# Cross-attention on one core: the order in which probabilities are split and multiplied by the values, and what the fill loads when

## The chip, the cores and the metric

The kernel runs on one core of a Trainium2 chip. The metric is the device time of one execution in microseconds (us). Five engines work side by side, each through its own instructions in the order in which they were issued: TensorE (PE, with its weight loads shown as PEld), VectorE (DVE), ScalarE (ACT), GpSimd (POOL) and SyncE (SP, which here issues nearly all DMAs). They wait for one another through semaphores.

## The reference

```python
q = heads(hidden @ to_q_w)                        # x: 32 batches x 512 rows x 640; 20 heads of 32
k, v = heads(ctx @ to_k_w), heads(ctx @ to_v_w)   # ctx: 32 x 77 keys x 1024
out = merge(softmax(q k^T / sqrt(32)) v) @ to_out_w + to_out_b + hidden
```

The other branches of the reference (object, other and image keys) have no keys in these inputs: all 77 keys are text. All is float32. The kernel splits each operand of a product into a high part in fp32r and the rest ("low") and adds three products: high by high, high by low, low by high.

## The kernel before

**Stages.** First all 32 batches' keys and values are computed and left in DRAM scratch (`k_dram`, `v_dram`), as are the split output weights (`wo_dram`). The main part then goes through 160 *slots*: slot `n = 5 b + j` handles batch `b` and a block `j` of four heads (128 of the 640 columns), for all 512 rows, in four row tiles `t`. After them, `end()` drains the pipeline. The order of all instructions is written by hand (`tc.manual_schedule`), so what `slot` says first is issued first on each engine. Buffers' waits are made by the tile pools.

**What a slot does.** It works for several heads blocks at once:

- PE: `scores(n, t)` for t = 0 to 3 (three matmuls each, tile `sc`), the queries of the next slot (`queries`, 15 matmuls, `pq`), the values product of slot `n - 4` (`values`, six matmuls of 512 columns, `pa`), and 24 output matmuls of an earlier batch in two *pieces* (`project` by `piece`, tile `po`). In slots with j = 1 and j = 4 the first piece stands before the fourth scores ("early").
- DVE: the negated maximum of the scores (`nm`, inside `scores`), `rest_p` (the low part of the probabilities, 128 x 1024), `sums` (the reciprocal `rs` of the softmax sums of slot n - 1), `low_a` (the low part of the attention output `at` of slot n - 5), `split_q`'s two low parts, the transposition `z` of the probabilities, the additions to the output (`finish`) and to `pa` (`sum_a`), transposes of the next batch's `x` (`xs`).
- ACT: `cast_p` (two casts of `raw` to the high part `pp`: 128 x 1024, and the last 64 key rows, 64 x 512), `high_a` (`at` high), four `exps` per row tile, `split_q`'s high part, `sum_a`'s copy, and casts of the next `x` (`split_x`).
- POOL: `copy_keys` (j = 1 and 4), `last_p` (low part of the last 64 rows, 64 x 512), `normalize` (multiplies the probabilities of slot n - 1 by `rs`, 128 x 1232), two casts of `split_q`, `add_bias`, low parts of `split_x`.
- SP: all loads and stores, among them `pd<-z` and its way back, `raw<-pd` (`load_p`), the keys (`load_keys`, `kb`), the values (`load_values`, `vb`), `x`, residuals and outputs. Each DMA of SP waits until the one issued eight before it has landed, as the build's order with its waits shows.

The probabilities take the way `pn` (exps, normalize), `z`, DRAM `pd`, `raw`, `pp`. A product of values reads `pp` in six passes: `pp[:, 0:2]` is the high part of 128 rows by two, `pp[:, 2:4]` their rest, and `pp[:, 4]` holds the high part of the last 64 rows in its lower half and the low part in its upper half.

The lines behind the steps below: L458, L462 and L464 `split_q`, L482 `scores`, L490 `nm`, L500 `exps`, L510 `sums`, L515 `normalize`, L522 `z`, L538 and L539 `load_p`, L546 and L547 `cast_p`, L553 `rest_p`, L560 `last_p`, L577 `values`, L588 and L590 `sum_a`, L597 `high_a`, L602 `low_a`, L621 `project`, L658 `finish`, L427 and L428 `copy_keys`, L447 `queries`, L264 and L265 `split_x`, L257 `transpose_x`, L412 the clearing of `vb`.

**The fill.** Slots 0 to 2 also carry the last value products of the context (`beside`). Slot 4 is the first that takes a product of values, slot 8 the first with output pieces. The order in a slot is this (cut):

```python
        if taken is not None:
            cast_p(taken)
        if n - 1 in takes:
            high_a(takes[n - 1])
        s = scores(n, 0)
        if taken is not None:
            rest_p(taken)
        rs = sums(n - 1) if n else None
        if taken is not None:
            last_p(taken)
        if n:
            normalize(n - 1, rs)
        if n - 1 in takes:
            low_a(takes[n - 1])
        exps(n, 0, *s)
        queries(n + 1, 0, 2)
        s = scores(n, 1)
```

Of the kernel before, what the change touches and what calls it, by code (L numbers as in the profile page):

```python
# [8 lines left out]
F32 = mybir.dt.float32  # L9
# [14 lines left out]
P = 128  # L24
# [27 lines left out]
def kernel(  # L52
# [325 lines left out]
    for round_ in (range(3), range(3, NC_)):  # L378
        for k in range(NK):
            for j in round_:  # L380
                keys(LAST, j, k)
        for j in round_:
            split_keys(LAST, j)
        if j == 2:
            load_x(1)
    psk.release()
# [10 lines left out]
    bias = main.tile([P, C], F32, name="bias")  # L397
    nc.sync.dma_start(bias, bo.unsqueeze(0).to_broadcast([P, C]))
    kbs, vbs, pnb = [], [], []
# [10 lines left out]
    for g, (j0, nj) in enumerate(GROUPS):  # L410
        vb = main.tile([P, nj, 2, 2, P], FPR, name=f"vb{g}")
        nc.gpsimd.memset(vb.bitcast(F32), 0.0)  # L412
        vbs.append(vb)
# [128 lines left out]
    def cast_p(n):  # L542

        raw = raws[n]
        pp = late[0].tile([P, 5, S], FPR, tag="pp", name="pp", bufs=1)
        nc.scalar.copy(pp[:, 0:2, :], raw[:, 0:2, :])  # L546
        nc.scalar.copy(pp[:64, 4, :], raw[:64, 2, :])  # L547
        pps[n] = pp

    def rest_p(n):  # L550

        raw, pp = raws[n], pps[n]
        nc.vector.tensor_tensor(  # L553
            pp[:, 2:4, :], raw[:, 0:2, :], pp[:, 0:2, :].bitcast(F32), ALU.subtract
        )

    def last_p(n):

        raw, pp = raws.pop(n), pps[n]
        nc.gpsimd.tensor_tensor(  # L560
            pp[64:, 4, :], raw[:64, 2, :], pp[:64, 4, :].bitcast(F32), ALU.subtract
        )

    PASSES = [(p, 0, p + c) for c in (0, 2) for p in range(2)] + [(p, 1, 4) for p in range(2)]

    def values(n, m0=0, m1=6):
        b, j = divmod(n, NC_)
        g = GROUP_OF[j]  # L570
        pp, vb = pps[n], vbs[g][:, j - GROUPS[g][0]]
        if m1 == 6:
            pps.pop(n)
        if m0 == 0:
            pas[n] = late[1].tile([P, 2, S], F32, tag="pa", name="pa", bufs=1)
        for p, t, c in PASSES[m0:m1]:
            nc.tensor.matmul(  # L577
# [3 lines left out]
                start=(c == p),  # L581
                stop=(t == 1),
            )
# [33 lines left out]

    def project(b, t, h, j, m0=0, m1=3):
        for m in range(m0, m1):
            a, c = PAIRS[m]  # L620
            nc.tensor.matmul(  # L621
# [5 lines left out]
            )  # L627

    def close_first(b, n):

        for m0, m1, v0, v1 in ((0, 2, 0, 4), (2, 3, 4, 6)):
            for h in range(2):
                project(b, 0, h, NC_ - 1, m0, m1)
            values(n, v0, v1)
        closed.extend(((b, 0, 0), (b, 0, 1)))

# [41 lines left out]

    WO = {1: (0,), 2: (1,), 3: (2,), 4: (3,), 5: (4,)}
    wos = []  # L680
# [22 lines left out]
    def slot(n, beside=()):  # L703
# [3 lines left out]
        bo_, has_out = b - back, b >= back  # L707
        xsplits = SPLIT_X.get(j, ((), ())) if more and n > 2 else ((), ())
        turns = TRANSPOSE_X.get(j, ((), (), ())) if more and b else ((), (), ())
        taken = takes.get(n)  # L710

        filling = taken is not None and not has_out
        if not filling:
            refill(b, j, 0)
        if j == 1:
            copy_keys(1)
        elif j == 4 and more:
            copy_keys(0)
        if taken is not None:
            cast_p(taken)  # L720
        if n - 1 in takes:
            high_a(takes[n - 1])
        bias_now = j in BIAS and b >= BIAS[j][0]
        if bias_now and not ahead:
            add_bias(b - BIAS[j][0], BIAS[j][1])
        s = scores(n, 0)
        if j == 2:
            finish()
        if taken is not None:
            rest_p(taken)  # L730
        rs = sums(n - 1) if n else None
        if taken is not None:
            last_p(taken)
        if n:
            normalize(n - 1, rs)
        if n - 1 in takes:
            low_a(takes[n - 1])
        exps(n, 0, *s)
        if ahead:
            queries(n + 1, 0, 2)  # L740
        s = scores(n, 1)
        if n >= LATE:
            load_p(n - LAG + 1)
# [16 lines left out]
        if not ahead:  # L760
            exps(n, 2, *s)
            close_first(bo_, taken)
            finish()
            s = scores(n, 3)
        early = ahead and has_out and j in (1, 4)
        if early:
            if j == 4:
                close_first(bo_, taken)
            else:
                piece(bo_, first)  # L770
            finish()
# [47 lines left out]
    def end():  # L819
# [8 lines left out]
        cast_p(N - 4)  # L828
        high_a(N - 5)
        rest_p(N - 4)  # L830
        transpose_p(N - 1)
        low_a(N - 5)
        last_p(N - 4)
        add_bias(last - 1, 2)
# [9 lines left out]
        def turn(n):  # L844
            sum_a(n)
            cast_p(n + 1)
            high_a(n)
            rest_p(n + 1)
            low_a(n)
            last_p(n + 1)  # L850

# [56 lines left out]

    load_keys(0, 0)
    copy_keys(0)  # L910
    queries(0, 0, NC_)
    split_q(0)
    context_values(LAST, 0, psv)
    for i in range(NQ):
        transpose_x(1, i)
    for c in range(2):
        split_x(1, c)
    context_values(LAST, 1, psv)
# [55 lines left out]
```

## Time and profile before

| | us |
|---|---|
| median of 3 runs | 1942.67 (1941.25 to 1948.3) |
| profiled execution | 1943.7, of which the span from first to last instruction is 1941.9 |
| PE busy | 1893.9 (98% of the span) |
| DVE, ACT, POOL busy | 1568.0, 1536.8, 1391.0 |
| mean granted TensorE clock | 0.994 |
| DMA | 431.37 MB, 222 GB/s on average |

In the page, "PE 1893.9 (98%)" means that matmuls were under way for 98% of the span. Matmul ends are modelled, and a matmul that starts late because its operand came late still lengthens what follows, so idle time alone understates what waiting costs. A slot's length is read from the timeline as the distance of the first matmul of `scores(n, 0)` from that of the next slot.

### The profile page before, as it was taken

What the parts mean: (1) busy time and instruction counts of PE and PEld (TensorE: products, weight loads), DVE (VectorE), ACT (ScalarE), POOL (GpSimd) and SP (SyncE); (2) the same over time, 40 slices, a digit from 0 to 9 for tenths busy, and PEclk for the clock granted to TensorE, in tenths of its full rate; (3) what the DMA queues carried; (4) which work ended last, traced back from release to release, by engine and by line L of the source; (5) the groups of instructions that cost most, each with busy time, mean ns of one, the idle gap of its engine ahead of it and who ended that gap; (6) DMA issues with size and microseconds to landing.
All of it is one profiled execution on the core that took longest, in us unless ns stands there. A gap on an engine that the chain in (4) does not pass through costs nothing. (4 is left out here: it accounts for less than half of the span.)

```text
span 1941.9 us, 37554 instructions
## 1 busy us (share of the span) xinstructions
PE 1893.9 (98%) x10332; PEld 1668.6 (86%) x10332; DVE 1568.0 (81%) x2494; ACT 1536.8 (79%) x6210; POOL 1391.0 (72%) x1116
## 2 busy tenths in 40 slices
PE   9999997999999999999999999999999999999998
PEld 7888885888888888888888888888888888888887
DVE  5444446888889888889889888888888888988885
ACT  3232247899988988888998889999989898898883
POOL 1100066888888888788887888888888888888883
PEclk9999998999999999999999999999999999999999
DMA  9888769888888888888888898888888888888875
GB/s 190 206 190 249 186 156 232 217 226 231 233 225 224 225 230 234 225 231 229 231 228 235 233 237 226 231 231 233 221 237 230 222 229 231 229 226 229 235 204 169
DMA packets 565023, 431.37 MB, mean 222 GB/s; under 512 B 191120, under 2 KB 473168, under 8 KB 564816
## 3 DMA queue, kind: packets, MB, share of 16 engines
q1 hardware_dynamic: 560304, 414.47, 82.8%
q0 software_dynamic: 4416, 14.34, 2.3%
q8 instruction: 85, 1.39, 0.3%
q14 instruction: 122, 1.00, 0.2%
q10 hardware_dynamic: 96, 0.16, 0.0%
HBM read 247.17 MB, written 181.64 MB: 221 GB/s over the span
## 5 line engine op out<-in xcount | busy, mean ns | idle before, releaser
L500 ACT ACTIVATE pn<-sc,nm 128x77 f32<-128x77 f32 x2560 | 802.0, 335 | 129.3 <-DVE nm L490 121.4
L621 PE MATMUL po<-wo_s,at 128*128 128x320 f32 x3840 | 637.6, 314 | 10.8 <-ACT at L597 9.8
L447 PE MATMUL pq<-xt,wq_s 128*128 128x512 f32 x2400 | 630.5, 402 | 3.3 <-POOL xt L265 0.2
L621 PEld LDWEIGHTS po<-wo_s,at 128*128 128x128 f32 x3840 | 571.3, 189 | 21.4 <-ACT at L597 15.2
L500 ACT ACTIVATION_READ_ACCUMULATOR pn<-sc,nm 128x1 f32 x2560 | 546.9, 214 | 0.0
L447 PEld LDWEIGHTS pq<-xt,wq_s 128*128 128x128 f32 x2400 | 428.1, 190 | 89.2 <-POOL xt L265 16.2
L515 POOL TENSOR_TENSOR pn<-pn,rs 128x1232 f32<-128x1232 f32 x160 | 363.9, 2274 | 53.5 <-DVE rs L510 43.3
L482 PEld LDWEIGHTS sc<-kb,qt 128*128 128x128 f32 x1920 | 329.4, 189 | 69.0 <-POOL qt L462 13.9
L560 POOL TENSOR_TENSOR pp<-raw,pp 64x512 fp32r<-64x512 f32 x160 | 290.6, 1816 | 131.2 <-ACT pp L547 112.8
L482 PE MATMUL sc<-kb,qt 128*128 128x154 f32 (+1 forms) x1920 | 323.4, 275 | 18.7 <-POOL qt L462 7.0
L464 DVE TENSOR_TENSOR qt<-pq,qt 64x512 fp32r<-64x512 f32 x320 | 220.2, 688 | 111.4 <-ACT qt L458 106.4
L490 DVE TENSOR_REDUCE nm<-sc 128x4 f32<-128x308 f32 x640 | 291.2, 459 | 19.8 <-PE sc L482 13.4
L577 PE MATMUL pa<-pp,vb 128*128 128x512 f32 x960 | 263.3, 404 | 8.1 <-DVE at L602 3.0
L522 DVE STREAM_TRANSPOSE z<-pn 128x1280 f32<-128x1280 f32 x160 | 241.8, 1511 | 8.6 <-DMA pd<-z 2.5
L590 DVE TENSOR_TENSOR pa<-pa,aw 64x512 f32<-64x512 f32 x320 | 222.5, 695 | 19.3 <-ACT aw L588 8.9
L553 DVE TENSOR_TENSOR pp<-raw,pp 128x1024 fp32r<-128x1024 f32 x160 | 203.7, 1273 | 32.6 <-ACT pp L546 32.4
L265 POOL TENSOR_TENSOR xt<-xs,xt 128x512 fp32r<-128x512 f32 x160 | 202.5, 1291 | 33.5 <-ACT xt L264 30.8
L462 POOL CAST qt<-qt 64x512 fp32r<-64x512 f32 x320 | 194.9, 609 | 31.9 <-ACT qt L458 14.1
L613 POOL TENSOR_TENSOR xr<-xr,bias 128x640 f32<-128x640 f32 x128 | 202.2, 1580 | 17.5 <-DMA xr<-in_x_dram 6.1
L577 PEld LDWEIGHTS pa<-pp,vb 128*128 128x128 f32 x960 | 171.9, 189 | 46.7 <-DVE at L602 15.1
L546 ACT CAST pp<-raw 128x1024 fp32r<-128x1024 f32 x160 | 168.7, 1055 | 42.7 <-DMA raw<-pd 40.9
L588 ACT COPY aw<-pa 64x1024 f32<-64x1024 f32 x160 | 161.9, 1012 | 20.1 <-PE pa L577 16.0
(46 smaller groups left out, 1594.0 us busy)
## 6 DMA issues: line engine op xcount, KB each, us to landing
pd<-z SPq DMA_DIRECT2D x640, 160.0 KB, 3.4
raw<-pd SPq DMA_DIRECT2D x160, 512.0 KB, 4.0
xs<-in_x_dram SPq DMA_DIRECT2D x128, 320.0 KB, 7.3
xr<-in_x_dram SPq DMA_DIRECT2D x128, 320.0 KB, 3.7
out_dram<-xr SPq DMA_DIRECT2D x127, 320.0 KB, 3.6
raw<-pd SPq DMA_DIRECT2D x160, 128.0 KB, 4.2
v_dram<-vs SPq DMA_DIRECT2D x80, 192.0 KB, 4.0
k_dram<-ks POOLq DMA_DIRECT2D x20, 512.0 KB, 4.4
```

The costliest lines, as they stand in the source:

```text
L447: nc.tensor.matmul(pqs[n], wq_s[:, k, a, j * P : (j + 1) * P], xts[b, k][:, c, :], start=(k == 0 and m == 0), stop=(k == NC_ - 1 and m == 2),)
L464: nc.vector.tensor_tensor(qt[r, 1 + w, :], pq[r], qt[r, 0, :].bitcast(F32), ALU.subtract)
L482: nc.tensor.matmul(sc[:, cols], qt[:, m, t * P : (t + 1) * P], keys_, start=(m == 0), stop=(m == 2),)
L490: nc.vector.tensor_reduce(nm, sc[:, :KCOLS].rearrange("p (h k) -> p h k", k=NKEY), AX.X, ALU.max, negate=True)
L500: nc.scalar.activation(pnb[n % 2][:, at, :NKEY], sc[:, i * NKEY : (i + 1) * NKEY], AF.Exp, bias=nm[:, i : i + 1], accum_out=sms[n][:, at : ...
L515: nc.gpsimd.tensor_tensor(pf, pf, rs.unsqueeze(2).to_broadcast([P, NQ * HPC, NKEY]), ALU.mult)
L522: nc.vector.transpose(z.rearrange("p b t j -> p t b j"), pn.rearrange("p (t h) k -> p t (h k)", t=NQ).rearrange("p t (b i) -> p t b i", i=Q),)
L553: nc.vector.tensor_tensor(pp[:, 2:4, :], raw[:, 0:2, :], pp[:, 0:2, :].bitcast(F32), ALU.subtract)
L560: nc.gpsimd.tensor_tensor(pp[64:, 4, :], raw[:64, 2, :], pp[:64, 4, :].bitcast(F32), ALU.subtract)
L577: nc.tensor.matmul(pas[n][:, p, :], vb[:, p, t, :], pp[:, c, :], start=(c == p), stop=(t == 1),)
L590: nc.vector.tensor_tensor(pa[64 * p : 64 * p + 64, 0], pa[:64, p], aw[:, p], ALU.add)
L621: nc.tensor.matmul(pos[b, t, h][:, :HALF], ats[b * NC_ + j][:, a, t * P : (t + 1) * P], wos[0][:, j, c, h * HALF : (h + 1) * HALF], start= ...
```

## The change

In every slot the last 64 rows of the probabilities are cast first (`cast_p`), their low part is taken before the rest of the 128-row part, and `rest_p` moves from before `sums` to after `scores(n, 1)`. The six passes of `values` go high, last rows, rest, where they went high, rest, last rows. `low_a` moves behind `rest_p`, except in slots with j = 4, where `high_a` is issued before `cast_p` and `low_a` before `scores(n, 1)`. `close_first`, which interleaved the two closing output products with the values product in those slots, is replaced by the piece and then the product. Slots without output issue `copy_keys` after `last_p`. In the fill, `x` of batch 1 is loaded after the first keys and is transposed and split within slots 0 to 3; the bias is loaded in slot 3; the five parts of the output weights come in slots 1 and 2 instead of 1 to 5; and `vb` is cleared after the first `copy_keys`. `end()` follows the new order of `last_p` and `rest_p`.

```diff
-        if j == 2:
-            load_x(1)
...
-    nc.sync.dma_start(bias, bo.unsqueeze(0).to_broadcast([P, C]))
...
-        nc.gpsimd.memset(vb.bitcast(F32), 0.0)
...
+        nc.scalar.copy(pp[:64, 4, :], raw[:64, 2, :])
         nc.scalar.copy(pp[:, 0:2, :], raw[:, 0:2, :])
-        nc.scalar.copy(pp[:64, 4, :], raw[:64, 2, :])
...
-    PASSES = [(p, 0, p + c) for c in (0, 2) for p in range(2)] + [(p, 1, 4) for p in range(2)]
+    PASSES = [(p, t, c + p * (t == 0)) for t, c in ((0, 0), (1, 4), (0, 2)) for p in range(2)]
...
-    def close_first(b, n):
-
-        for m0, m1, v0, v1 in ((0, 2, 0, 4), (2, 3, 4, 6)):
-            for h in range(2):
-                project(b, 0, h, NC_ - 1, m0, m1)
-            values(n, v0, v1)
-        closed.extend(((b, 0, 0), (b, 0, 1)))
...
-    WO = {1: (0,), 2: (1,), 3: (2,), 4: (3,), 5: (4,)}
+    WO = {1: (0, 1, 2), 2: (3, 4)}
...
-        xsplits = SPLIT_X.get(j, ((), ())) if more and n > 2 else ((), ())
-        turns = TRANSPOSE_X.get(j, ((), (), ())) if more and b else ((), (), ())
+        xsplits = SPLIT_X.get(j, ((), ())) if more else ((), ())
+        turns = TRANSPOSE_X.get(j, ((), (), ())) if more else ((), (), ())
...
-        if j == 1:
-            copy_keys(1)
-        elif j == 4 and more:
-            copy_keys(0)
-        if taken is not None:
+        copied = {1: 1, 4: 0 if more else None}.get(j)
+        if has_out and copied is not None:
+            copy_keys(copied)
+        if taken is not None and j != NC_ - 1:
             cast_p(taken)
         if n - 1 in takes:
             high_a(takes[n - 1])
+        if taken is not None and j == NC_ - 1:
+            cast_p(taken)
...
         s = scores(n, 0)
         if j == 2:
             finish()
-        if taken is not None:
-            rest_p(taken)
         rs = sums(n - 1) if n else None
         if taken is not None:
             last_p(taken)
+        if not has_out and copied is not None:
+            copy_keys(copied)
         if n:
             normalize(n - 1, rs)
-        if n - 1 in takes:
-            low_a(takes[n - 1])
         exps(n, 0, *s)
         if ahead:
             queries(n + 1, 0, 2)
+        if j == NC_ - 1 and n - 1 in takes:
+            low_a(takes[n - 1])
         s = scores(n, 1)
+        if taken is not None:
+            rest_p(taken)
+        if j != NC_ - 1 and n - 1 in takes:
+            low_a(takes[n - 1])
+        if n == LATE:
+            nc.sync.dma_start(bias, bo.unsqueeze(0).to_broadcast([P, C]))
...
         if early:
+            piece(bo_, first)
             if j == 4:
-                close_first(bo_, taken)
-            else:
-                piece(bo_, first)
+                values(taken)
             finish()
...
     load_keys(0, 0)
+    load_x(1)
     copy_keys(0)
+    for vb in vbs:
+        nc.gpsimd.memset(vb.bitcast(F32), 0.0)
     queries(0, 0, NC_)
     split_q(0)
     context_values(LAST, 0, psv)
-    for i in range(NQ):
-        transpose_x(1, i)
-    for c in range(2):
-        split_x(1, c)
     context_values(LAST, 1, psv)
```

## The prediction

> **What bounds the kernel now.** I read the page's busy line first, then the windows by stage, then the timeline of single slots on each engine.
>
> ```profile
> PE 1893.9 (98%) x10332; PEld 1668.6 (86%) x10332; DVE 1568.0 (81%) x2494; ACT 1536.8 (79%) x6210; POOL 1391.0 (72%) x1116
> 250.00:300.00 50.00, 45.86 (x232) 41.78 (x232) 24.82 (x43) 22.99 (x120) 32.17 (x41) 0.97 0.71 178
> 300.00:350.00 50.00, 35.29 (x145) 27.30 (x144) 35.35 (x54) 39.14 (x167) 32.99 (x29) 0.86 0.95 222
> 1050.00:1100.00 50.00, 49.50 (x282) 43.86 (x281) 44.35 (x71) 45.01 (x189) 40.51 (x33) 1.00 0.87 229
> ```
>
> TensorE is the bound (columns of a window: PE, PEld, DVE, ACT, POOL busy, clock, DMA share, GB/s). Only the fill around 300 us has an idle PE. In the steady part DVE, ACT and POOL are 81 to 90% busy, so they have about a microsecond a slot to spare.
>
> Slot lengths from the timeline show what the steady part still wastes: means over slots 10 to 154 are 9.84, 9.85, 9.96, 9.99 and 11.30 us for j = 0 to 4, though the PE work is the same in each. A cycle of five slots is 50.93; five times 9.84 is 49.20. So 1.73 us a cycle is waiting, 1.46 of it in j = 4. Slot 79 (starts at 1072.26) shows where:
>
> ```profile
> 1077.80 0.85 PE L621 MATMUL po<-wo_s,at 128*128 128x320 f32 x4 [0.27 <-ACT at L597]
> 1078.78 1.20 PE L577 MATMUL pa<-pp,vb 128*128 128x512 f32 x4
> ```
>
> The closing output product waits for `high_a`, issued behind both casts, and the values product for `low_a`.
>
> **What the change removes.** In j = 4 `high_a` goes ahead of the casts (1.05 + 0.63 us) and `low_a` ahead of `rest_p`: both waits of slot 79 go, as does a wait of some 0.3 us for `split_x`'s last POOL part if POOL runs earlier. Cover for all: 1.73 us a cycle, about 29 cycles, 50 us. Nothing in the count of matmuls changes.
>
> **What it puts in their place: POOL against `rest_p`.** Both work SBUF to SBUF, and the trace shows that they exclude each other:
>
> ```profile
> 1045.02 1.29 POOL L560 TENSOR_TENSOR pp<-raw,pp 64x512 fp32r<-64x512 f32 x1
> 1045.69 1.70 DVE L553 TENSOR_TENSOR pp<-raw,pp 128x1024 fp32r<-128x1024 f32 x1
> 1086.16 2.39 POOL L560 TENSOR_TENSOR pp<-raw,pp 64x512 fp32r<-64x512 f32 x1 [0.99 <-ACT pp L547]
> 1086.20 1.21 DVE L553 TENSOR_TENSOR pp<-raw,pp 128x1024 fp32r<-128x1024 f32 x1
> ```
>
> In the first pair `last_p` began first and `rest_p` took 1.70 instead of 1.21; in the second `rest_p` got hold and `last_p` took 2.39 instead of 1.29. Before, `rest_p` always ran ahead of `sums`, so `normalize`, 2.27 us, could never be under way when it started. Now `sums` comes first. Slot 77 (j = 2, starts at 1052.24), before:
>
> ```profile
> 1055.94 0.43 DVE L490 TENSOR_REDUCE nm<-sc 128x4 f32<-128x308 f32 x1
> 1056.30 0.46 DVE L658 TENSOR_TENSOR xr<-po,xr 128x320 f32<-128x320 f32 x1
> 1056.70 1.21 DVE L553 TENSOR_TENSOR pp<-raw,pp 128x1024 fp32r<-128x1024 f32 x1
> 1057.83 0.24 DVE L510 RECIPROCAL rs<-sm 128x16 f32<-128x16 f32 x1
> 1058.00 0.62 DVE L602 TENSOR_TENSOR at<-pa,at 128x512 fp32r<-128x512 f32 x1
> 1058.54 0.46 DVE L490 TENSOR_REDUCE nm<-sc 128x4 f32<-128x308 f32 x1
> 1055.53 1.30 POOL L560 TENSOR_TENSOR pp<-raw,pp 64x512 fp32r<-64x512 f32 x1 [2.15 <-ACT pp L547]
> 1058.22 2.27 POOL L515 TENSOR_TENSOR pn<-pn,rs 128x1232 f32<-128x1232 f32 x1 [1.39 <-DVE rs L510]
> ```
>
> Rebuilt in the new order: the reciprocal follows `finish`, 1056.70 to 1056.94; `normalize` starts 0.15 later as in these rows, 1057.09 (`last_p` ended at 1056.83 and is now earlier); the next maximum is done at 1057.32, and only then can `rest_p` start. POOL is ahead by 0.23 us. `rest_p` waits until about 1059.25, ends at 1060.45, `low_a` behind it at 1061.0, and the values product, which needs the old `pa` read, starts at 1061.06. PE wants it 6.32 after the slot's start (slots 80 and 81), at 1058.56. That is 2.5 us. The maximum of `scores(n, 1)` is no longer behind `rest_p`, so ACT's wait of 1.4 us for it in this slot goes and the chain runs some 0.5 us earlier: 2.0. Bounds: 0, if `last_p` lasts long enough that `rest_p` goes first, to 2.5. `last_p` now starts after the second `raw` DMA, issued 2.8 us before this slot (1049.45) and on average 4.2 us under way by the page's DMA part, so it ends 3.5 us into the slot, before `rest_p` can start (5.1 here, 4.6 in a chain 0.5 earlier). I take 2.0.
>
> No row shows `rest_p` against `normalize`; the nearest is `last_p` against it, 0.5 us for the 0.62 that `last_p` still had to go. The Trainium skill (SBUF — State Buffer, "Who interferes with whom") says that a DVE instruction with two SBUF inputs and a GpSimd instruction that reads SBUF share a port, and that whoever starts first keeps it for the whole instruction. By that rule the full 2.0 is paid. Going by the rows alone, with a block no longer than `last_p` (1.28 instead of 2.27), it would be 1.0; I take the longer one, since the rows show a wait that lasts as long as the other instruction does.
>
> The same race in the other slots, by rows of slots 78 to 81:
> - j = 0: maximum and reciprocal done 2.84 into slot 80, `normalize` possible at 3.0, `rest_p` at 3.2: 0.7 us lost, unless POOL's bias addition (1.57) runs later with a shorter j = 4 and puts `last_p` over the gap. I take 0, up to 0.7.
> - j = 1: POOL waits for keys (1.2 us idle, `copy_keys`), `last_p` lasts to 4.3 and `rest_p`, ready at 3.9, comes next: 0, up to 1.6 if keys land early.
> - j = 3: `last_p` follows `split_x` on POOL and covers `rest_p`'s start; `low_a` is late by 0.8 from today's rows, 0 if all runs 1 us earlier. I take 0.
> - j = 4: PE wants the two passes of the last rows at 5.9 into the slot, right after the high ones; before, they came last, at 7.9 in slot 79. POOL first does `split_x` (to 4.2) and `copy_keys` (0.57 + 0.84), then `last_p`, 1.28: 6.9. If `rest_p` slips in between (casts end at 5.5), 7.9. With POOL a microsecond earlier, 6.9: a wait of 1.0. Bounds 0.4 to 2.0.
>
> A stall of 2.0 us can also cost clock. In the last slot PE idled 1.33 and 0.73 us within 3 us, and the next window (1890 to 1895) was granted 0.66, 1.7 us lost; 0.80 us alone at 1902.9 cost nothing. I charge one stall in five, 0.35 a cycle, bounds 0 and 1.7. The Trainium skill (TensorE: Matmul & The Clock Gate, "What's actually happening") wants an idle window of about 3.4 us before the clock halves; by that rule this term is 0 and the total 10 us less.
>
> Sum of a cycle: 2.0 (j = 2) + 1.0 (j = 4) + 0.35 - 1.73 = +1.62; times 29, +47 us. The j = 2 race will not go the same way each time (landing times of `raw` vary): at 17 in 20 of its cost, -9 us, **+38**.
>
> **The fill and the end.** The first scores waited 3.55 us for keys queued behind `x` of batch 1 (four DMAs of 320 KB). With keys first they land some 4 us earlier, but the clearing of `vb` (1.38 + 0.96) now stands on POOL before `split_q`'s casts: -2. In slots 4 to 7 three weight transfers of 640 KB leave a DMA share of 0.95, where PE once waits 5.5 us for exps behind late `raw` and `x`: -5. Against it, five of them in slots 1 and 2 delay `pd` and `raw(0)`, and two `split_x` on POOL come before slot 3's casts: +2. Fill -5, bounds -12 and +5. The bias in slot 3, 0.68 us on SP, is hidden: its first addition is in slot 12. The last slot and `end()`: `high_a` earlier saves up to 2, `last_p` against `rest_p` gives it back: -1, bounds -4 and +2.
>
> From the profiled 1943.7: +38 - 5 - 1 = 1975.7; the median of the runs lies 1.0 below it: **1975 us**.
>
> **The rivals.**
> - *The race goes to `rest_p`* (faster). If the second `raw` DMA lands a microsecond later or DVE runs earlier, `last_p` still holds POOL when `rest_p` gets ready. The point is 0.23 us in slot 77: POOL later by more than that. Then j = 2 costs nothing, j = 4 about 0.9: 0.9 - 1.73, times 29, -24, with the fill -30: 1913. For it: ACT waited for `raw` in 43 slots, 40.9 us in all, and only the first half was waited for.
> - *Mixed* (no change). Lost in a third of the cycles: 0.7 + 1.0 - 1.73 = 0; fill -6: 1937.
> - *Lost in j = 0, 1 or 3 too*: about 4.5 a cycle, +2.8, times 29, +81, less 6: 2018. For it: in slots 78 and 80 today's rows give 0.8 and 0.7. Against: each PE stall gives POOL and DVE time to catch up.
>
> **How the numbers follow.** Forecast 0.50, lost more often 0.16, race to `rest_p` 0.22, mixed 0.12. The forecast's own range is 1950 to 2000. To hold 8 in 10 the range must reach the centre of the faster rival and past that of the costlier one: 1912 to 2025. About 0.5%, 10 us, can be told from no change. Faster takes the faster rival and a little of the mixed one, 0.23; same 0.11; slower 0.66.
>
> **What would show it.** In the changed trace: mean of L553 well above 1273 ns (near 2000), with `rest_p` rows of 3 us or more where L515 began just before; PE's values product waiting for L602 in j = 2 slots; in j = 4 no wait for L597 but one for L560, with L560's mean below 1816; j = 2 slots near 11.5 us and j = 4 near 10.8. The first scores at about 262, no 5.5 us wait near 330. If L553 keeps its mean, or j = 2 stays at 9.85, the forecast is wrong and the time is near 1913.

## The result, and the profile after

The changed kernel takes **1923.69 us** (median of 4 runs, 1921.87 to 1924.51) against 1943.56 us for the kernel before (4 runs, 1941.25 to 1948.3): a ratio of 0.9893, 95% interval 0.9873 to 0.9914. The forecast was 1975, slower. The profiled execution took 1923.57 us, its span 1921.7.

The busy line of the page, after:

```profile
PE 1883.1 (98%) x10332; PEld 1665.2 (87%) x10332; DVE 1626.7 (85%) x2494; ACT 1526.3 (79%) x6210; POOL 1422.3 (74%) x1116
```

The same three stretches in the windows view, after (columns as before):

```profile
250.00:300.00 50.00, 46.36 (x244) 42.34 (x242) 26.35 (x46) 25.06 (x128) 34.06 (x43) 1.00 0.80 217
300.00:350.00 50.00, 39.78 (x166) 31.80 (x167) 40.83 (x59) 41.83 (x178) 37.21 (x32) 0.86 0.87 195
1050.00:1100.00 50.00, 49.88 (x286) 44.35 (x285) 46.60 (x73) 45.01 (x191) 43.02 (x34) 1.00 0.86 229
```

PE is now at work for 39.78 us of the fill's worst stretch instead of 35.29. The count of instructions is the same. DVE and POOL are busier by 58.7 and 31.3 us, and that is waiting for each other that counts as busy, as the groups below show. The span is 20.1 us shorter, and slots 10 to 154 tell where that came from (means in us, from the timeline of one execution each):

| | j = 0 | 1 | 2 | 3 | 4 | cycle |
|---|---|---|---|---|---|---|
| before | 9.83 | 9.85 | 9.96 | 9.99 | 11.29 | 50.91 |
| after | 9.84 | 10.04 | 10.06 | 10.23 | 10.15 | 50.32 |

Slot 10 starts 4.7 us earlier, slots 10 to 154 save 17.3 us (29 times 0.60), and what follows slot 154 takes 1.9 us more. So j = 4 gains 1.14 a cycle and j = 1 to 3 give 0.54 of it back.

The groups of instructions after, for the three instructions that the forecast set against each other (busy us, mean ns of one | idle before them):

```profile
L511 POOL TENSOR_TENSOR pn<-pn,rs 128x1232 f32<-128x1232 f32 x160 | 503.5, 3147 | 23.8 <-DVE rs L506 12.3
L549 DVE TENSOR_TENSOR pp<-raw,pp 128x1024 fp32r<-128x1024 f32 x160 | 261.1, 1632 | 31.0 <-ACT pp L543 24.9
L556 POOL TENSOR_TENSOR pp<-raw,pp 64x512 fp32r<-64x512 f32 x160 | 212.4, 1327 | 97.5 <-ACT pp L542 88.5
```

`normalize` is the one that waits: 3147 ns where it took 2274. `rest_p` waits only for what `last_p` has left (1632, was 1273). Slot 77, the one that the forecast rebuilt, starts at 1042.15; the timeline of DVE and POOL:

```profile
1046.24 0.23 DVE L506 RECIPROCAL rs<-sm 128x16 f32<-128x16 f32 x1
1046.39 0.41 DVE L486 TENSOR_REDUCE nm<-sc 128x4 f32<-128x308 f32 x1
1046.61 3.45 POOL L511 TENSOR_TENSOR pn<-pn,rs 128x1232 f32<-128x1232 f32 x1 [0.55 <-DVE rs L506]
1046.73 1.20 DVE L549 TENSOR_TENSOR pp<-raw,pp 128x1024 fp32r<-128x1024 f32 x1
```

`normalize` starts 0.12 us ahead of `rest_p`, yet `rest_p` takes its undisturbed 1.20 us and `normalize` ends 2.13 us after it, nearly its whole own time of 2.27. In slots 10 to 154 `rest_p` went ahead of `normalize` 145 times out of 145. In 41 of them `normalize` had started first: 26 in j = 0, 14 in j = 2, one in j = 1. In the other 15 slots with j = 2 `rest_p` started first as well, by 0.01 to 0.53 us.

The other way round is seen once, in the fill (slot 5), where the maximum started 0.41 us after DVE had become free, since it waited for PE:

```profile
319.48 2.27 POOL L511 TENSOR_TENSOR pn<-pn,rs 128x1232 f32<-128x1232 f32 x1 [0.22 <-DVE rs L506]
319.75 0.48 DVE L486 TENSOR_REDUCE nm<-sc 128x4 f32<-128x308 f32 x1 [0.41 <-PE sc L478]
320.14 2.69 DVE L549 TENSOR_TENSOR pp<-raw,pp 128x1024 fp32r<-128x1024 f32 x1
```

In j = 4 (slot 79, starts at 1062.43) neither `high_a` nor `last_p` is waited for:

```profile
1066.57 1.29 POOL L556 TENSOR_TENSOR pp<-raw,pp 64x512 fp32r<-64x512 f32 x1
1066.79 2.15 DVE L549 TENSOR_TENSOR pp<-raw,pp 128x1024 fp32r<-128x1024 f32 x1 [0.37 <-ACT pp L543]
1066.95 1.09 PE L613 MATMUL po<-wo_s,at 128*128 128x320 f32 x6
1067.88 1.85 PE L570 MATMUL pa<-pp,vb 128*128 128x512 f32 x6
```

`last_p` starts 4.13 us into the slot and ends at 5.42; the forecast had 6.9. DVE had stood still for 0.37 us here, and it is `rest_p` that is held: 2.15 us instead of 1.2.

### The profile page after: what moved, and what is told of

The parts are those of the page before. It is cut to its first block, busy times and chain, and to the rows that moved or that the text cites. A ratio compares the mean times of both kernels' runs of the same rounds, so it can differ in the third digit from the quotient of the medians.

```text
span 1921.7 us, 37548 instructions
## 1 busy us (share of the span) xinstructions
PE 1883.1 (98%) x10332; PEld 1665.2 (87%) x10332; DVE 1626.7 (85%) x2494; ACT 1526.3 (79%) x6210; POOL 1422.3 (74%) x1116
## 4 chain that ended last, share of the span: by engine, by line
PE 44%; ACT 15%; DVE 14%; DMA 13%; issue 5%; SPq 5%; POOL 3%; DVEq 0%; POOLq 0%; ACTq 0%
PE pq L443 11%; PE po L613 11%; PE pv L191 6%; DMA raw<-pd 6%; ACT pn L496 6%; PE pk L191 6%; PE pa L570 5%; PE sc L478 4%; DVE pp L549 4%; DMA xs<-in_x_dram 3%; ACT pp L543 2%; DVE nm L486 2%; DVE z L518 2%; ACT xt L264 2%; ACT aw L581 2%
## 5 line engine op out<-in xcount | busy, mean ns | idle before, releaser
L496 ACT ACTIVATE pn<-sc,nm 128x77 f32<-128x77 f32 x2560 | 794.0, 333 | 32.6 <-DVE nm L486 27.7
L443 PE MATMUL pq<-xt,wq_s 128*128 128x512 f32 x2400 | 621.4, 400 | 0.0
L511 POOL TENSOR_TENSOR pn<-pn,rs 128x1232 f32<-128x1232 f32 x160 | 503.5, 3147 | 23.8 <-DVE rs L506 12.3
L478 PE MATMUL sc<-kb,qt 128*128 128x154 f32 (+1 forms) x1920 | 317.9, 274 | 13.8 <-POOL qt L458 8.9
L549 DVE TENSOR_TENSOR pp<-raw,pp 128x1024 fp32r<-128x1024 f32 x160 | 261.1, 1632 | 31.0 <-ACT pp L543 24.9
L556 POOL TENSOR_TENSOR pp<-raw,pp 64x512 fp32r<-64x512 f32 x160 | 212.4, 1327 | 97.5 <-ACT pp L542 88.5
L542 ACT CAST pp<-raw 64x512 fp32r<-64x512 f32 x160 | 99.5, 622 | 97.6 <-DMA raw<-pd 97.3
```

The lines of the kernel that those rows point to most:

```text
L443: nc.tensor.matmul(pqs[n], wq_s[:, k, a, j * P : (j + 1) * P], xts[b, k][:, c, :], start=(k == 0 and m == 0), stop=(k == NC_ - 1 and m == 2),)
L478: nc.tensor.matmul(sc[:, cols], qt[:, m, t * P : (t + 1) * P], keys_, start=(m == 0), stop=(m == 2),)
L496: nc.scalar.activation(pnb[n % 2][:, at, :NKEY], sc[:, i * NKEY : (i + 1) * NKEY], AF.Exp, bias=nm[:, i : i + 1], accum_out=sms[n][:, at : ...
L511: nc.gpsimd.tensor_tensor(pf, pf, rs.unsqueeze(2).to_broadcast([P, NQ * HPC, NKEY]), ALU.mult)
L549: nc.vector.tensor_tensor(pp[:, 2:4, :], raw[:, 0:2, :], pp[:, 0:2, :].bitcast(F32), ALU.subtract)
```

## The experiments

Every ratio is to the kernel before, run beside it on the same chip; the chips differ between groups of experiments. Slot lengths and waits are those of one profiled execution of each kernel, and the executions of one kernel differ by up to about 1%.

### What the parts give

**Slots alone, fill alone.** One kernel has the fill hunks undone, the other only those done (x of batch 1, bias, weights, `vb`, key copies).

> The changed order of the slots and of end(), with the fill as it was before (x of batch 1 loaded and split ahead of slot 0, bias at the start, weights in slots 1 to 5, values cleared early, key copies first). The traces split the gain of 20.2 us into 4.7 before slot 10, 17.3 in slots 10 to 154, and a loss of 1.9 after them. Theory 1 (parts add up; j = 4 pays for everything): slots 10 to 154 keep their 17.3 us, cycle 50.3, j = 4 near 10.15; total about 15 us under the kernel before, 1928. Theory 2 (the phase in which the steady part runs comes from the fill, so the race for SBUF in the slots goes the other way without it): rest_p is held up behind normalize in j = 2, its mean is near 2000 ns or more instead of 1632, and the time is near or above the kernel before, 1940 to 1975.

> The fill of the changed kernel, with the slots and end() as before. Theory 1: only the 4.7 us before slot 10 are saved, or somewhat less because part of them came from the new order in slots 4 to 9; cycle 50.9 as before, total 3 to 5 us under the kernel before, 1939 to 1941. Theory 2 (the fill sets the phase): slots 10 to 154 move too, by more than 5 us either way.

> The changed kernel unaltered, on the chip on which its variants run: the slots alone were 0.9937 of the kernel before there, the fill alone 0.9995. Theory 1 (the parts add): 0.993 here, so the 0.9893 of the first comparison is not reached on every chip. Theory 2 (the fill sets the phase in which DMAs land in all later slots): 0.989 again, which the two parts (0.9937 by 0.9995) don't give, and j = 1 and j = 3 slots at 10.0 and 10.2 where the slots alone had 10.24 and 10.55.

Slots alone: 0.9937 (0.9916 to 0.9958), 10 to 12 us less than the kernel before where Theory 1 had 15; its profiled execution, the longest of 11, has a cycle of 50.97, so it doesn't show where they come from. `rest_p` has a mean of 1597 ns there, so Theory 2 fell. Fill alone: 0.9995 (0.9979 to 1.0011). The unaltered changed kernel, on a further chip: 0.9923 (0.9905 to 0.9940). The parts add within the intervals; the fill's 4.7 us of the first traces is not seen as time by itself. Nor is it steady: slot 10 began at 369.92 us in this further run of the unaltered kernel, 0.4 us ahead of the kernel before, and between 365.4 and 371.3 in the other kernels below that have the new fill. The gain lies in the slots.

**A square of two edits.** On the kernel before: attention first in j = 4, `rest_p` behind `scores(n, 1)`, or both.

```diff
+        if taken is not None and j == NC_ - 1:   # attention first: high_a, then cast_p
+            cast_p(taken)
...
-        if taken is not None:                    # rest late: from ahead of sums
-            rest_p(taken)
...
         s = scores(n, 1)
+        if taken is not None:                    # to here, low_a behind it
+            rest_p(taken)
```

> The kernel before with one edit: in slots with j = 4 high_a is issued ahead of the casts and low_a ahead of rest_p. Casts, passes, rest_p's place, close_first and the fill stay as before. Theory 1 (the whole gain is the two waits of j = 4): j = 4 falls from 11.30 to 10.1 to 10.2 us, the other slots stay at 9.84 to 9.99, cycle 49.8, 29 cycles by 1.15 us = 33 us less: about 1910, better than the changed kernel by some 13. Theory 2 (j = 4 needs the last rows early as well: cast, low part and passes): last_p still starts 6.3 us into the slot behind the second cast and rest_p, the two passes of the last rows wait for it until about 7.6, and j = 4 falls only to 10.7 or so: cycle 50.3, about 1926.

> The kernel before with one edit: rest_p and low_a stand behind scores(n, 1), so sums come first, in all slots; j = 4 keeps its casts ahead of high_a and its low_a behind rest_p. It is the fourth corner of a square: neither edit 1, attention first in j = 4 alone 1.0017, both 0.9906. Theory 1 (each alone moves j = 4's wait from one operand to the next, and only both take it away): high_a is still behind the casts in j = 4 and low_a gets later still, j = 4 stays at 11 us or more, and the time is 1.00 or above. Theory 2 (sums ahead of rest_p, and POOL earlier by it, is the whole gain): j = 4 falls to 10.6 here too, 0.991.

> The kernel before with attention first in j = 4 and, in all slots, rest_p behind scores(n, 1) (so sums ahead of it); casts, passes, close_first, end() and fill as before. Attention first alone gave nothing: 1.0017 of the kernel before. Theory 1 (what j = 4 needs is POOL earlier: sums ahead of rest_p starts normalize of j = 2 to 4 about 1.2 us earlier, so that split_x, copy_keys and last_p no longer stand behind it): j = 4 falls from 11.16 to 10.3 or less, and the time to 0.994 of the kernel before. Theory 2 (the last rows first, in cast and passes, are needed too): last_p behind the later cast starts normalize late again, j = 4 stays at 11 us, and the time is within 0.3% of the kernel before or above.

| | rest_p ahead of sums | rest_p late |
|---|---|---|
| j = 4 as before | 1 | 0.9935 (0.9915 to 0.9956) |
| attention first | 1.0017 (1.0001 to 1.0034) | 0.9906 (0.9887 to 0.9925) |

The three ratios come from three chips. Attention first by itself gives nothing: j = 4 falls only to 11.16, less than either theory had, since the values product now waits for `rest_p` and then `last_p`, which POOL starts 5.6 us into the slot. `rest_p` late gives about two thirds by itself, where Theory 1 had nothing and Theory 2 nearly all; its trace has a cycle of 50.87, and no trace of the kernel before from that chip stands beside it, so the slots that gained can't be told.

The edit does two things at once. It brings `sums` forward, and with it `normalize`, which starts 3.62 us into a slot with j = 0 instead of 5.05 (medians over slots 10 to 154). And it frees the maximum behind `rest_p`. From ACT's view of the waits, the exps' wait for the maximum in the kernel before (us in all, times, longest):

```profile
ACT pn L500 <- DVE nm L490: 121.4, 188, 1.9
```

and with `rest_p` late alone:

```profile
ACT pn L500 <- DVE nm L490: 46.3, 113, 1.9
```

With attention first alone it is 107.6 us, with both 58.8, in the changed kernel 27.7. This wait falls with the edit, but it does not rank the kernels: those with 58.8 us (both edits) and 60.5 (last rows last, below) are no slower than the one with 27.7. No run moves `sums` without freeing the maximum, so which of the two brings the gain is not shown. What goes with them is an earlier POOL: ahead of slot 79 `normalize` of j = 3 ends 2.29 us before the slot starts in the changed kernel, 1.04 before; `split_x` and `copy_keys` of j = 4 stand some 1.26 us earlier in the slot, and `last_p` 2.1, since before, the second copy of keys ran beside `rest_p` and took 1.46 us instead of 0.57.

**The last rows' order.** Large cast first and passes high, rest, last: in all slots; or, in two mixed kernels, with the last rows first in j = 4 alone, in cast and passes or in the cast only.

> The changed kernel with the last rows last again: the large cast first, and the passes of values high, rest, last. All else as changed. Theory 1 (the last rows' early cast lets last_p, and with it normalize, start about 1.05 us earlier, by the large cast's length): last_p and normalize start up to 1 us later in j = 1 to 3, rest_p meets last_p or gets ahead of it, which makes last_p 2.3 us; 5 to 20 us slower than the changed kernel, 0.995 to 1.003 of the kernel before. Theory 2 (POOL is what last_p waits for, in j = 3 and 4, and raw's second DMA in j = 1 and 2, so the order of the casts moves nothing): within 0.2% of the changed kernel, 0.992.

> The changed kernel with the last rows first (cast and passes) only in the product that slots with j = 4 take; in the other slots the large cast first and the passes high, rest, last, as before. With the last rows last everywhere the slots took 9.84, 9.87, 9.99, 9.91 and 10.60 us, in the changed kernel on the same chip 9.85, 10.08, 10.05, 10.31 and 10.19. Theory 1 (each order is better in its own slots, and they don't disturb one another): the cycle is 9.84 + 9.87 + 9.99 + 9.91 + 10.19 = 49.80, 0.4 by 29 = 12 us less than with the last rows last everywhere: 0.982 of the kernel before, faster than both kernels. Theory 2 (j = 4 gains at the cost of its neighbours: POOL's and DMA's phase moves with it): j = 4 stays at 10.4 to 10.6 or j = 1 to 3 go up by as much, 0.988 to 0.992.

> The changed kernel with the passes high, rest, last in every slot, and the small cast first only for the product that slots with j = 4 take. The mixed run before had the passes high, last, rest in j = 4: there last_p started 0.16 us after rest_p (4.55 against 4.39), took 2.2 us, and the third pass waited for it until 6.76, so j = 4 took 11.22; j = 0 to 3 took 9.86, 9.85, 9.94 and 9.89. Theory 1 (with the last rows at the end, two passes of rest_p, done at 5.6, fill that wait): the last two passes are wanted at 6.4 and come at 6.8, j = 4 at 10.2 to 10.3, cycle 49.8: 0.982 of the kernel before. Theory 2 (the slots before take what j = 4 saves, since a longer j = 4 only lets DVE and POOL catch up): j = 4 near 10.6 as with the last rows last everywhere, 0.988 to 0.991.

Last rows last everywhere: 0.9885 (0.9866 to 0.9905), slots of 9.84, 9.87, 9.99, 9.91 and 10.60; on the same chip the changed kernel, in another group, had 0.9923. Theory 1 had it 5 to 20 us slower than the changed kernel, Theory 2 equal. So last rows first, as a part of the change, gains nothing; in the traces it takes 0.4 us off j = 4 and puts 0.7 on j = 1 to 3. Neither mixed kernel adds up the better halves; the ratios are in the ranges of Theory 2, with a longer j = 4 than it had: 0.9909 (0.9894 to 0.9924) with j = 4 at 11.22, and 0.9883 (0.9857 to 0.9909) with j = 4 at 10.91. Slot 79 of the first mixed kernel shows why; the timeline:

```profile
1070.08 1.23 DVE L550 TENSOR_TENSOR pp<-raw,pp 128x1024 fp32r<-128x1024 f32 x1 [0.37 <-ACT pp L544]
1070.24 2.20 POOL L557 TENSOR_TENSOR pp<-raw,pp 64x512 fp32r<-64x512 f32 x1
1072.49 1.21 PE L574 MATMUL pa<-pp,vb 128*128 128x512 f32 x4 [0.73 <-POOL pp L557]
```

POOL ends the copies of keys 0.42 us later in the slot than in the changed kernel, `rest_p` is first, `last_p` takes 2.20 us, and PE waits 0.73 us for it. The two lowest ratios, 0.9883 and 0.9885, can't be told from the changed kernel's 0.9893 of the first comparison; that one of these orders beats it is not shown.

**rest_p ahead of sums again**, in all slots of the changed kernel, or in j = 0 to 2.

```diff
+        if taken is not None:        # or: and j < 3
+            rest_p(taken)
         rs = sums(n - 1) if n else None
...
```

Not shown here: `rest_p` leaves its place behind `scores(n, 1)` in these slots.

> The changed kernel with rest_p back ahead of sums (its place before), so that normalize cannot be under way when rest_p starts; last rows first, j = 4 attention first and the fill stay as changed. Theory 1 (what the changed kernel loses in j = 1 to 3, 0.19 + 0.10 + 0.24 us a cycle against before, is low_a late behind rest_p, which stands behind the maximum of scores(n, 1)): these come back, cycle 49.8, 0.5 us by 29 = 15 us less than the changed kernel, about 1909. Theory 2 (rest_p ahead of the maximum makes ACT wait for it again, 121 us in all before against 28 in the changed kernel, and the chain of exps, queries' split and z gets later): j = 4 goes back above 10.5 and the total is 1925 to 1940.

> The changed kernel with rest_p ahead of sums in slots with j = 0, 1 and 2 only; j = 3 and 4 as changed. In the run with rest_p ahead of sums everywhere, j = 1 and 2 took 9.85 and 9.87 us, against 10.04 and 10.06 in the changed kernel, and all its loss sat in j = 3 (10.52) and j = 4 (13.64). Theory 1 (that loss is low_a queued behind rest_p in j = 4 itself): j = 3 and 4 stay at 10.2, the cycle falls by 0.38 us to 49.9, 29 times that is 11 us: 0.994 of the changed kernel. Theory 2 (sums behind rest_p starts normalize late, and POOL hands its delay on to the next slots, where split_x, copy_keys and last_p get late): normalize in j = 2 starts about a microsecond later, j = 3 and 4 lengthen by 0.3 to 0.6 us each, and the time is that of the changed kernel or up to 25 us above.

In all slots: 1.0416 (1.0390 to 1.0441). In j = 4 `low_a` then stands behind `rest_p` and both casts, PE's output product waits for it (87.6 us in 62 waits, the longest 3.1), and j = 4 takes 13.64. In j = 0 to 2 only: 0.9981 (0.9963 to 0.9999). Against the unaltered kernel on that chip `normalize` of j = 1 starts 6.17 us into the slot instead of 4.84, ACT's wait for maxima is 58.4 us instead of 29.7, and j = 1 takes 10.53. That j = 1 and 2 took 9.85 in the first of these runs probably came from the time that its long j = 4 gave the other engines; the second run, with the same order in j = 0 to 2 and a j = 4 of 10.22, speaks for it. Theory 1 fell both times. Theory 2 had the first run at 1925 to 1940, where it took 2030; in the second it had the total, but j = 3 and 4 did not lengthen.

**Attention first in all slots**, then with `copy_keys` behind `last_p` in j = 4 as well.

```diff
-        if taken is not None and j != NC_ - 1:
-            cast_p(taken)
         if n - 1 in takes:
             high_a(takes[n - 1])
-        if taken is not None and j == NC_ - 1:
+        if taken is not None:
             cast_p(taken)
...
```

Not shown here: `low_a` goes ahead of `scores(n, 1)` in all slots as well.

> The changed kernel with the order of j = 4 in every slot: high_a ahead of the casts and low_a ahead of scores(n, 1), so low_a no longer stands behind rest_p. Theory 1 (what j = 1 to 3 still waste is low_a late behind rest_p; PE waited for it in 16 places, 9 us, and the values product started 0.2 to 0.4 us late in j = 2 and 3): j = 1 to 3 fall to 9.9, cycle 49.9, 12 us less than the changed kernel, 0.994 of it. Theory 2 (high_a waits for sum_a's last addition, done 2.66 us into a slot, and holds up the casts behind it on ACT, by 0.6 us in j = 2 and 3 and up to 1.2 in j = 0): casts, last_p, rest_p and the exps of the second row tile get late, the two last passes wait for rest_p, and it is 5 to 20 us slower than the changed kernel.

> The kernel with attention first in all slots, and in slots with j = 4 copy_keys behind last_p on POOL instead of ahead of it. With attention first everywhere, j = 0 to 3 took 9.85 us each and j = 4 took 11.64, where last_p, behind the copies, started 0.08 us after rest_p, took 2.27 us and kept the two passes of the last rows waiting for 1.44 us. Theory 1 (that race is j = 4's loss): last_p starts when its cast ends, 4.1 us into the slot, ends at 5.4, rest_p at 6.6, no pass waits; j = 4 at 10.2, of which 0.4 stay for the late split_x; cycle 49.6, 0.7 by 29 = 20 us less than the changed kernel: 0.982 of the kernel before. Theory 2 (the copies behind last_p delay normalize in j = 4 or the keys that the next slot's first scores read): the loss moves to j = 0, 0.5 us or more, and the time is that of the changed kernel.

1.0007 (0.9996 to 1.0018) and 0.9974 (0.9961 to 0.9987). The first brings j = 0 to 3 to 9.86, 9.85, 9.85 and 9.86, nearly without waits, and puts all of it into j = 4 (11.64), where `rest_p` starts 0.09 us ahead of `last_p` and the passes wait 1.04 us. The second moves the wait on to j = 0 (10.86), for `split_q`'s casts behind `normalize`, which now ends 0.30 us ahead of that slot (1.82 in the first). So in both runs what some slots gained, another paid for, and in the second Theory 2 held. POOL is 84% busy between 370 and 1850 us in the first, waits for DVE included; that it has too little time left over a cycle is the likely reason, not a shown one.

### The race of j = 2

**A memset, and a second maximum, ahead of `rest_p`**, to give `normalize` a longer lead (the time by which it starts ahead of `rest_p`). The second maximum stands in every slot with j = 2 and output.

```diff
         s = scores(n, 1)
+        if j == 2 and has_out and b % 6:
+            nc.vector.memset(idle[:, : 100 * (b % 6)], 0.0)   # or the maximum of s[0] again
         if taken is not None:
             rest_p(taken)
```

> The changed kernel with a DVE memset of 0, 100, 200, 300, 400 or 500 columns (by batch modulo 6; 512 columns took 485 ns in the profile) just ahead of rest_p in slots with j = 2, so that normalize is ahead of rest_p by more than the 0.12 us that the changed kernel shows at most there. Theory 1 (the forecast's lock exists, but POOL needs a lead of more than 0.12 us and less than the 0.66 us of slot 5, the one row in which rest_p took 2.69 us): from 200 or 300 columns on, rest_p takes 2.9 to 3.3 us instead of 1.2, low_a ends near 8.0 us into the slot, the values product waits for it by 1.5 to 2 us, in some 17 slots: about 30 us slower than the changed kernel. Theory 2 (rest_p always goes first whatever the lead, and slot 5 had another cause): rest_p stays at 1.2 us, slots lengthen by no more than the memset, 0.1 to 0.5 us: under 8 us in all.

> The changed kernel with the maximum of scores(n, 1) taken a second time into a spare tile, just ahead of rest_p in slots with j = 2. It reads PSUM, where the memset of the run before wrote SBUF and held normalize up by its own length. One such maximum takes 0.40 to 0.48 us, so rest_p gets ready some 0.33 later and normalize is ahead by 0.45 instead of 0.12. Theory 1 (the forecast's lock and price were right, only its lead was not: normalize loses at 0.12 and has it from 0.25 on, as in three rows of the runs so far, leads 0.252, 0.254 and 0.287, rest_p 3.07 to 3.10 us): rest_p takes about 3.0 us in 15 to 20 of the 29 slots, low_a ends 8.2 to 8.6 us into the slot, the values product waits 1.8 to 2.2 us: 30 to 45 us slower than the changed kernel, 1.008 to 1.015 of the kernel before. Theory 2 (DVE, once busy, keeps the port from POOL whatever it does): rest_p stays at 1.2 us, slots lengthen by 0.35 us at most, under 10 us in all.

0.9935 (0.9911 to 0.9958) and 1.0010 (0.9994 to 1.0025). `rest_p` went first in every one of these slots, with leads of `normalize` up to 0.65 and 0.50 us. One row of the second maximum:

```profile
1052.02 3.84 POOL L512 TENSOR_TENSOR pn<-pn,rs 128x1232 f32<-128x1232 f32 x1 [0.50 <-DVE rs L507]
1052.14 0.46 DVE L729 TENSOR_REDUCE spare<-sc 128x4 f32<-128x308 f32 x1
1052.52 1.21 DVE L550 TENSOR_TENSOR pp<-raw,pp 128x1024 fp32r<-128x1024 f32 x1
```

Theory 2 held for the race: leads up to 0.65 us do not decide it. `normalize` got next to nothing done in its lead: where it started first, it ended 2.13 to 2.14 us after `rest_p` in every row. Time was lost to the delay: j = 2 took 10.15 and 10.37 instead of 10.05 on the same chip. The second run lost about 16 us against the changed kernel's ratio on that chip, more than the 10 that Theory 2 allowed; 0.3 a cycle sits in j = 2, 0.14 in j = 1.

**A pause of DVE ahead of `rest_p`**, by a small copy that waits for an exponential.

```diff
+        if j == 2 and has_out:
+            nc.vector.tensor_copy(spare, pnb[n % 2][:, HPC - 1, :HPC])
         if taken is not None:
             rest_p(taken)
```

> The changed kernel with one small copy on DVE just ahead of rest_p in slots with j = 2, which reads four columns of the last exponential of the first row tile, so DVE pauses until ACT has written it, about 5.1 us into the slot, while normalize starts at 4.5. In all runs so far normalize went first in 7 rows, with a lead of 0.14 to 0.66 us and a maximum that started up to 0.41 us after the reciprocal's end, and rest_p went first in 265 rows, with leads up to 0.65, where DVE ran without a break. Theory 1 (a pause of DVE is what gives POOL the port; the forecast's price holds once it has it): rest_p takes 2.7 to 3.1 us, ends near 8.0, low_a near 8.6, the values product waits some 2.2 us in most of the 29 slots: 50 to 70 us slower than the changed kernel, 1.02 of the kernel before. Theory 2 (rest_p goes first here too): it takes 1.2 us from 5.2 on, low_a ends at 7.1, the product waits 0.6: 15 to 20 us slower than the changed kernel, 1.001.

1.0400 (1.0374 to 1.0426). Now POOL keeps what it has. Slot 77 (starts at 1088.50), timeline:

```profile
1092.94 2.28 POOL L512 TENSOR_TENSOR pn<-pn,rs 128x1232 f32<-128x1232 f32 x1
1094.07 1.17 DVE L729 COPY spare<-pn 128x4 f32<-128x4 f32 x1 [0.94 <-ACT pn L497]
1095.15 1.21 DVE L550 TENSOR_TENSOR pp<-raw,pp 128x1024 fp32r<-128x1024 f32 x1
1097.07 2.15 PE L571 MATMUL pa<-pp,vb 128*128 128x512 f32 x6 [2.10 <-issue]
```

The copy of four columns is held for 1.17 us, until `normalize` ends; `rest_p` and `low_a` follow, and PE idles 2.10 us before the values product. So here it is the copy that waits, and of the 2.10 us some 0.94 are the pause itself. j = 2 takes 13.45 us, 3.4 more than in the changed kernel.

`rest_p` itself was held in slots with j = 3 of the same run. Slot 78, where the maximum had waited 0.27 us for PE:

```profile
1104.88 2.28 POOL L512 TENSOR_TENSOR pn<-pn,rs 128x1232 f32<-128x1232 f32 x1
1104.91 3.33 DVE L550 TENSOR_TENSOR pp<-raw,pp 128x1024 fp32r<-128x1024 f32 x1
```

In slots 10 to 154 there are 12 such rows, `rest_p` 3.3 us with a lead of 0.04 us or less; these slots took 10.43 to 10.47 us and the other slots with j = 3 9.85 to 9.95, also the three of them (18, 88, 133) that follow a j = 2 as long as most of the 12 do. There the lost race cost 0.6 us. What it would cost in j = 2 without a pause, where the forecast had 2.0, no run shows.

The windows view of the microseconds after the wait in slot 77 (PE, PEld, DVE, ACT, POOL busy, clock, DMA share, GB/s):

```profile
1097.00:1098.00 1.00, 0.93 (x4) 0.84 (x5) 1.00 (x2) 0.00 (x0) 0.92 (x2) 0.97 0.92 155
1098.00:1099.00 1.00, 1.00 (x4) 0.73 (x3) 0.97 (x3) 0.88 (x6) 1.00 (x1) 0.50 0.89 344
1099.00:1100.00 1.00, 1.00 (x6) 0.98 (x5) 0.54 (x2) 0.97 (x6) 0.15 (x1) 0.50 1.09 284
1100.00:1101.00 1.00, 1.00 (x5) 1.00 (x5) 0.97 (x2) 1.00 (x2) 0.96 (x1) 0.50 0.47 83
```

The clock is granted at half for three microseconds after the wait.

**The same race in the kernel before.** The trace that the forecast was made from has it between `last_p` and `rest_p`. Slot 66:

```profile
944.22 2.86 POOL L560 TENSOR_TENSOR pp<-raw,pp 64x512 fp32r<-64x512 f32 x1 [0.40 <-ACT pp L547]
944.72 1.19 DVE L553 TENSOR_TENSOR pp<-raw,pp 128x1024 fp32r<-128x1024 f32 x1
```

`last_p` starts 0.50 us ahead, and `rest_p` still takes its 1.2 us while `last_p` waits. There are 49 such rows, with leads of `last_p` from 0.02 to 0.57 us, all in a DVE stream without a break; in 15 rows, with leads from 0.55 to 0.98 us, `last_p` kept what it had and `rest_p` waited.

## Why the prediction was wrong

- **What bounds the kernel, and the 1.73 us a cycle to be had**: right in the count; j = 4 held nearly all of it, and 1.14 came off there.
- **The j = 2 race, +2.0 a cycle: the step that failed.** It rested on `normalize` being 0.23 us ahead of `rest_p`, and on the one that starts first keeping the shared port. In 15 of the 29 slots `rest_p` started first; in the other 14 the lead of `normalize` is 0.11 to 0.12. The rebuilt chain added whole durations, where the rows of a DVE that runs on start 0.07 to 0.08 us before the one ahead has ended. But the lead is not what failed: with 0.50 and 0.65 us `rest_p` went first too. j = 2 cost 0.10, not 2.0. The trace of before could have told: of the two pairs that the forecast shows, the second has `last_p` start first, at 1086.16 against 1086.20, and lose, and 0.23 lies well inside the leads of the 49 rows like it. The Trainium skill (SBUF — State Buffer, "Who interferes with whom") says that issue order decides who blocks; the forecast took the start shown in the trace for the issue, and if the rule holds, these rows say that the two are not the same. The rival "the race goes to `rest_p`" was right in its outcome; its condition, POOL later by 0.23 us, was not needed.
- **Removing rest_p from ahead of the maximum** was credited with 0.5 us in one slot. The edit that does it is the main gain: by itself 0.9935, with ACT's wait for maxima down from 121.4 to 46.3 us and `normalize` earlier. Which of these two brings the gain is open. The forecast took the change's name, attention first, for its worth; alone that gave nothing (1.0017).
- **j = 4, +1.0 for the wait for `last_p`**: 0.0 for `last_p`; the fifth pass waits for `rest_p` instead and starts 0.41 us after the fourth, where others stand 0.23 apart: 0.2. The step let `rest_p` slip in ahead of `last_p` (7.9) and took off a microsecond for an earlier POOL (6.9). Measured, `split_x` ended at 2.91 instead of 4.2, both copies of keys took 0.57, and `last_p` began 0.22 us ahead of `rest_p` and was done at 5.42, before PE wanted it.
- **j = 0, 1 and 3, taken as 0**: 0.0, +0.19 and +0.25, within their bounds. `low_a` behind `rest_p` is late there: with `low_a` ahead of it (attention first in all slots) j = 1 and 3 take 9.85 and 9.86. In j = 0 `normalize` started first in 26 of 29 slots, and there too nothing was lost.
- **Clock, +0.35**: nothing here, since no wait over 1.5 us is left between 400 and 1800 us; where a run had one of 2.1 to 2.5 us, it cost about 1.5 us in seven slots of ten, so one stall in five was too few for the case that this term was meant for.
- **The signs it named**: the mean of `rest_p` rose (1632 ns) and that of `last_p` fell (1327), but the first came from `last_p`, not from `normalize`; after the fill no `rest_p` row reaches 2.4 us, and j = 2 took 10.06, not 11.5.
- **The sum**: -1.14 + 0.10 + 0.19 + 0.25 = -0.60 a cycle, where the forecast had +1.62; 29 times the difference is 64 us. The profiled time lies 52 us below the forecast's 1975.7, since the forecast had taken 9 off for races won and the end is 3 worse than it said.
- **The fill, -5**: the first scores at 262.2 (forecast 262), the 5.5 us wait gone, slot 10 earlier by 4.7; but that is no more than executions differ by, and the fill alone gave 0.9995, about 1 us. **The end, -1**: +1.9.

## What to carry to other kernels

Two instructions that exclude each other are not ordered by which starts first in the trace: look in many rows for the one that ends as if it were alone, and at whether its engine had paused before it. Here two rows were read where 64 stood in the trace. Before pricing a moved instruction, list what stood queued behind it: here a reciprocal and a 0.43 us maximum, for which POOL and ACT waited, and bringing them forward was worth more than the waits that the change was named after. A better order of one slot is only a gain if the other slots of the cycle don't pay for it.

## What the runs showed of the hardware

- **Who gets the port.** In the runs' traces there are 335 rows in which `normalize` started before `rest_p`, by up to 1.77 us, and `rest_p` followed a maximum. `rest_p` went first in 307. In 305 of these, with leads up to 0.12 us, the maximum took 0.403 to 0.412 us, so DVE had run on without a break; in two it took 0.48 and the lead was 0.012 us or less. `normalize` went first in 28, and in 27 of these the maximum took 0.449 to 0.480 us, so DVE had stood still or nearly so; there a lead of 0.017 us was enough. With `last_p` in the kernel before, an unbroken DVE kept `rest_p` first up to a lead of 0.57 us and lost from 0.55 on. So the start in the trace is not the moment that decides: in an unbroken stream `rest_p` was decided for earlier, by up to 0.57 us there and 0.65 behind the memset. By how much, differs: in the changed kernel `last_p` went first with leads of 0.32 and 0.41 us in an unbroken stream too. That a pause of DVE lets POOL in is shown for the copy by the run that forced it; for `rest_p` it is read from rows as they fell, those of j = 3 in the same run above all. What DVE does in an unbroken stream that keeps POOL out before `rest_p` starts stays open; in the kernel before, `normalize` ran its 2.27 us beside an unbroken DVE with no `rest_p` next in line.
- **The clock after one wait.** A slot with one PE wait of 2.07 to 2.55 us was longer than the mean of such slots in the changed kernel by the wait and a further 1.3 to 2.0 us in 36 of 50 slots of two runs (`rest_p` ahead of sums, DVE pause), and by the wait alone, within 0.1 us, in the other 14. With one wait of about 1.04 us in each j = 4 slot (attention first in all slots) the granted clock stayed at 1.00. The Trainium skill (TensorE: Matmul & The Clock Gate, "What's actually happening") asks for an idle window of about 3.4 us; the rows say that a single wait of 2.1 us can be enough, and that it isn't each time.
